# In the attention's steps, the products for the next row maxima follow the scores directly, and the values follow both

## The chip, the cores and the metric

The kernel runs on one core of one Trainium2 chip. The time is device microseconds of that core. A core has five engines that work side by side and each take their own instructions in order: TensorE (PE, matrix products, into PSUM), VectorE (DVE), the scalar engine (ACT), GpSimd (POOL) and the queue that starts copies (SP). [...]

## The reference

Two layers of a metaformer run over x of shape 2 x 256 x 64 x 64: attention by areas, a recurrence over 4096 tokens, a mixer, and eight experts. The change lies in the first of these parts. With the normalisations of the batch left out, it computes

```python
# x: (2, 256, 64, 64), normalised over channels; 4 areas of 1024 positions per image,
# 8 heads of 32 channels each
attn = jnp.einsum('bhdn,bhdm->bhnm', q, k) * hd ** (-0.5)
attn = jax.nn.softmax(attn, axis=-1)
o = jnp.einsum('bhdm,bhnm->bhdn', v, attn)
...
return _conv1x1_bn(o + pp, w_proj, pr_g, pr_b, pr_m, pr_v)   # pp: a 5 x 5 convolution of v, by channel
```

and adds the result to x. The softmax takes the maximum of each row off before the exponential.

## The kernel before

`area_attention` treats 8 areas (2 images x 4) of 1024 positions, each in two groups of four heads: 16 groups, `GROUPS`. A group has 16 steps (`t`), two halves `n` of 512 queries times 8 blocks `m` of 128 keys; the loop at L542 runs over all 256. The order of the instructions on each engine is written out by hand (`manual_schedule`): what the loop emits first runs first.

A step of the loop emits, in this order:

- `scores` (L347): for four heads side by side on TensorE, each on 32 of its 128 rows, a product that puts minus the row maximum in (L352) and the scores on top of it (L357). They land in two wide tiles, s0 for heads 0 and 1, s1 for heads 2 and 3. ACT then takes the exponential of each (L364), into SBUF.
- `values` (L374) of the step before (`pending`): its exponentials times v, by four heads side by side on TensorE's columns (L370), summed over 8 steps in the tile `av_o`. After the eighth, ACT copies the sum (L383).
- small works from the table `SMALL`: `place` (L290) at steps 1 and 9 (other steps in the first group) turns the maxima found, split into three bf16 parts by `join`, into rows with a product (L294), an ACT copy (L298) and four copies on the SP queue (L301).
- `maxima` (L265), ahead of time for the next group (for the one after it in the last two steps): four products of the same shape as the scores but with queries on the output's partitions (L270), in two wide tiles m0 and m1. VectorE reduces each to row maxima (L275). The table `AHEAD` has one such set a step, `AHEAD_FIRST` two in the first ten steps of group 0.
- a sum of two exponential tiles on POOL (L564), by which the softmax's sums need fewer products. It carries two dependencies by hand: on the last product of the `maxima` and on the VectorE operation that was marked last before them.
- taps of the 5 x 5 convolution on VectorE (L324), as many as `TAPS` says for the step.
- from the tables `MINE` and `AROUND` projections for the next groups, averages, transposes and the output (L166, L178, L239), which use a PSUM tile `po` with one buffer; `sums` (L385) in every fourth step; and from `LATE` and `LATE_AROUND` the vector work of the normalisation and of `join`. The normalisation's root takes a power on POOL (L203) in step 6 of an area's first group.

The wide tiles are two PSUM banks each and come from one pool with three buffers, which `scores` and `maxima` take in turn:

```python
ps1 = ctx.enter_context(tc.tile_pool(name="a_psum_1", bufs=3, space=PSUM))
...
def wide():
    return ps1.tile([P, 2, 512], F32, name="ps", tag="ps")
```

The exponentials' tiles have three buffers in even steps and one in odd steps (L363).

Of the kernel before, what the change touches and what calls it, by code (L numbers as in the profile page):

```python
# [93 lines left out]
def area_attention(tc, sh, ap):  # L94
# [13 lines left out]
    with ExitStack() as ctx:  # L108
# [39 lines left out]
        def wide():  # L148
            return ps1.tile([P, 2, 512], F32, name="ps", tag="ps")
# [108 lines left out]
        def head(h):  # L258
            return slice(HD * h, HD * h + HD)
# [5 lines left out]
        def maxima(G, at):  # L265

            i, n = CHUNKS[at]
            tiles = [wide(), wide()]
            for h in range(GH):
                mm = nc.tensor.matmul(  # L270
                    tiles[h // 2][:, h % 2], qs[G, i // HM][head(h), i % HM * P : (i % HM + 1) * P],
                    ks[G, n][head(h)], start=True, stop=True, tile_position=(HD * h, 0),
                )
            for j in range(2):
                nc.vector.tensor_reduce(  # L275
                    nms[G][:, n, 2 * j : 2 * j + 2, i], tiles[j], AX.X, ALU.max, negate=True
                )
            return mm.ins
# [27 lines left out]
        def taps(A):  # L306

            vh, a = vhs[A], AREAS[A][1]
            for lower in range(2):
                for c in range(2):  # L310
                    if not lower:
                        acc = accs[A, c] = p1.tile([P, AROWS, WW], F32, name=f"acc{c}")
                        nc.vector.tensor_scalar(
                            acc, vh[:, c, 2 : 2 + AROWS], w_pe[:, c, 12:13], t_pe[:, c : c + 1], ALU.mult, ALU.add
                        )
                        yield
                    for k in range(25):
                        dy, dx = k // 5 - 2, k % 5 - 2
                        if dy == 0 and dx == 0 or (dy > 0) != lower:
                            continue  # L320
                        r0, r1 = window(dy, AROWS, AROWS * a, HH)
                        w0, w1 = window(dx, WW)
                        part = accs[A, c][:, r0:r1, w0:w1]
                        mark(nc.vector.scalar_tensor_tensor(  # L324
                            part, vh[:, c, 2 + r0 + dy : 2 + r1 + dy, w0 + dx : w1 + dx],
                            w_pe[:, c, k : k + 1], part, ALU.mult, ALU.add,
                        ))
                        yield
# [18 lines left out]
        def scores(G, n, m):  # L347

            tiles, k = [wide(), wide()], ks[G, m // HM]
            for h in range(GH):  # L350
                at = slice(HD * h, HD * h + 3)
                nc.tensor.matmul(  # L352
                    tiles[h // 2][:, h % 2], ones_b[at], mxs[G, n][at],
                    start=True, stop=False, tile_position=(HD * h, 0),
                )
            for h in range(GH):
                nc.tensor.matmul(  # L357
                    tiles[h // 2][:, h % 2], k[head(h), m % HM * P : (m % HM + 1) * P], qs[G, n][head(h)],
                    start=False, stop=True, tile_position=(HD * h, 0),
                )  # L360
            exs = []
            for i in range(2):
                exs.append(pe.tile([P, 2, 512], F32, name=f"ex{i}{m % 2}", bufs=1 if m % 2 else 3))  # L363
                nc.scalar.activation(exs[i], tiles[i], AF.Exp, scale=HD**-0.5)  # L364
            return exs
# [3 lines left out]
        def on_columns(to, h, lhs, exs, first, last):  # L369
            nc.tensor.matmul(  # L370
                to[head(h)], lhs, exs[h // 2][:, h % 2], start=first, stop=last, tile_position=(0, HD * h)
            )

        def values(G, n, m, exs):  # L374
            A, c = GROUPS[G]
            if m == 0:
                values_of[0] = ps2.tile([P, 512], F32, name="av_o")
            for h in range(GH):
                on_columns(values_of[0], h, vts[A, c][:, m, head(h)], exs, m == 0, m == NM - 1)
            if m == NM - 1:  # L380
                if n == 0:
                    ys[A, c] = p3.tile([P, NA], F32, name="y")
                nc.scalar.copy(ys[A, c][:, HALVES[n]], values_of[0])  # L383

        def sums(G, n, half, pairs):  # L385

            ps = bank()
            for i, exs in enumerate(pairs):
                for h in range(GH):
                    on_columns(ps, h, ones, exs, i == 0, i == len(pairs) - 1)  # L390
            if half == 0:
                held["sum"] = p1.tile([P, 512], F32, name="sum")
                nc.scalar.copy(held["sum"], ps)
                return

            y, total = ys[GROUPS[G]][:, HALVES[n]], held.pop("sum")
            nc.vector.tensor_tensor(total, total, ps, ALU.add)
            turned = p1.tile([P, 512], F32, name="turned")
            nc.vector.transpose(turned, total)
            small = p1.tile([P, 512 // 32], F32, name="small")  # L400
            nc.vector.reciprocal(small, turned.rearrange("p (k i) -> p k i", i=32)[:, :, 0])
            nc.vector.transpose(
                total.rearrange("p (k i) -> p k i", i=32), small.unsqueeze(2).to_broadcast([P, 512 // 32, 32])
            )
            mark(nc.vector.tensor_tensor(y, y, total, ALU.mult))
# [123 lines left out]
        def works(G, t, *tables):  # L529

            A, c = GROUPS[G]
            mine, around = tables
            plan = [(f, G + k, a, len(GROUPS)) for k, f, *a in mine.get(t, ())]
            plan += [(f, A + k, a, len(AREAS)) for k, f, *a in around.get(t, ())]
            for f, at, a, end in plan:
                if 0 <= at < end:
                    f(at, *a)

        pending, due, pairs, odd = None, {}, [], None
        at_end = mybir.DependencyInfo(mybir.DependencyClass.Sync, mybir.DependencyReason.DATA)  # L540
        conv = iter(())
        for g in range(16 * len(GROUPS)):  # L542
            G, t = divmod(g, 16)
            A, c = GROUPS[G]
            n, m = divmod(t, NM)
            new = G == 0
            if t == 0 and c == 0:
                conv = taps(A)
            exs = scores(G, n, m)
            if pending is not None:  # L550
                values(*pending)
            works(G, t, SMALL_FIRST if new else SMALL, {})

            mm, before = None, latest[0]
            for k, at in (AHEAD_FIRST if new else AHEAD).get(t, ()):
                if G + k < len(GROUPS):
                    mm = maxima(G + k, at)
            pair = None
            if m % 2:
                pair = (pairs[-1][0], exs[0])  # L560
            elif odd is not None:
                pair = (pairs[-1][1], odd)
            if pair is not None:
                add = nc.gpsimd.tensor_tensor(pair[0], *pair, ALU.add)  # L564
                if mm is not None:
                    tc.add_manual_dep(add.ins, mm.name, at_end, reason="beside the reductions")
                    tc.add_manual_dep(add.ins, before.name, at_end, reason="beside the reductions")
            for _ in range((TAPS_FIRST if A == 0 else TAPS)[c][t]):
                next(conv, None)
            works(G, t, FIRST if new else MINE, AROUND[c])  # L570
            if g in due:
                sums(*due.pop(g))
            works(G, t, LATE_FIRST if new else LATE, LATE_AROUND_FIRST if new else LATE_AROUND[c])
            pending = G, n, m, exs
            if m % 2:
                odd = exs[1]
                if m % 4 == 3:
                    due[g + 2] = G, n, m // 4, pairs
                    pairs = pairs[-1:]
            else:  # L580
                pairs = (pairs if m % 4 else []) + [exs]
# [1677 lines left out]
```

## Time and profile before

| what | us |
|---|---|
| median of 2 runs (3005.82 and 3010.76) | 3008.29 |
| the profiled execution, its own time | 3003.18 |
| span of its instructions | 3001.4 |
| steps of the attention, from the first L352 to the end of the last step | about 63 to 1465 |
| recurrence, mixer and experts | from about 1498 on |

The profile gives for each engine a record of every instruction. A group of equal instructions is named by its line, its engine and its tiles, "written<-read"; PEld is the weight load that goes ahead of a product. An fp32 product stands there as two records, two passes. The view of waits names who waited for whom; idle time of an engine costs something only where the end depends on it. TensorE's ends are modelled, so the distance from one start to the next is safer to read than a length.

### The profile page before, as it was taken

What the parts mean: (1) busy time and instruction counts of PE and PEld (TensorE: products, weight loads), DVE (VectorE), ACT (ScalarE), POOL (GpSimd) and SP (SyncE); (2) the same over time, 40 slices, a digit from 0 to 9 for tenths busy, and PEclk for the clock granted to TensorE, in tenths of its full rate; (3) what the DMA queues carried; (4) which work ended last, traced back from release to release, by engine and by line L of the source; (5) the groups of instructions that cost most, each with busy time, mean ns of one, the idle gap of its engine ahead of it and who ended that gap; (6) DMA issues with size and microseconds to landing.
All of it is one profiled execution on the core that took longest, in us unless ns stands there. A gap on an engine that the chain in (4) does not pass through costs nothing. (4 is left out here: it accounts for less than half of the span.)

```text
span 3001.4 us, 45442 instructions
## 1 busy us (share of the span) xinstructions
PE 2724.7 (91%) x17798; PEld 1512.9 (50%) x17798; DVE 2173.2 (72%) x3227; ACT 1348.5 (45%) x2417; POOL 1358.1 (45%) x1037
## 2 busy tenths in 40 slices
PE   7999999999999999998689999968887499999994
PEld 2222232333323333322189999953444378888872
DVE  4799898999989999998766667779987812222116
ACT  3344444454544445444344455556753822222223
POOL 1444545554454555546523000038773256666651
PEclk9999999999999999999899999989999799999995
DMA  3000000000000000000023000005552456666658
GB/s 127 1 1 1 1 1 1 1 1 1 1 1 1 1 1 1 2 1 1 2 104 148 1 2 1 1 24 152 149 141 57 166 184 230 228 224 228 225 178 339
DMA packets 58659, 220.34 MB, mean 73 GB/s; under 512 B 14440, under 2 KB 15344, under 8 KB 48704
## 3 DMA queue, kind: packets, MB, share of 16 engines
q0 software_dynamic: 25440, 125.24, 11.7%
q1 hardware_dynamic: 31760, 87.82, 8.9%
q10 hardware_dynamic: 1232, 4.25, 0.4%
q8 instruction: 142, 2.33, 0.3%
q14 instruction: 85, 0.70, 0.1%
HBM read 173.30 MB, written 43.58 MB: 72 GB/s over the span
## 5 line engine op out<-in xcount | busy, mean ns | idle before, releaser
L564 POOL TENSOR_TENSOR ex<-ex,ex 128x1024 f32<-128x1024 f32 x255 | 617.3, 2425 | 615.1 <-PE ps L270 248.9
L275 DVE TENSOR_REDUCE nm<-ps 128x2 f32<-128x1024 f32 x512 | 601.3, 1219 | 91.2 <-PE ps L270 90.5
L364 ACT ACTIVATE ex<-ps 128x1024 f32<-128x1024 f32 x512 | 498.0, 1022 | 318.2 <-PE ps L357 285.5
L324 DVE SCALAR_TENSOR_TENSOR acc<-vh,w_pe,acc 128x1008 f32<-128x1008 f32 (+7 forms) x384 | 548.9, 1431 | 7.1
L270 PE MATMUL ps<-k,q 32*128 32x512 f32 x2048 | 348.0, 647 | 4.9 <-DVE nm L275 3.6
L2003 DVE COPY xt<-px 128x512 f32<-128x512 f32 x68 | 47.0, 692 | 398.0 <-PE px L2001 398.0
L2015 ACT ACTIVATE act<-ph,wt 128x256 f32<-128x256 f32 x272 | 128.8, 474 | 395.8 <-PE ph L2013 373.0
L2013 PE MATMUL ph<-xt,wt 128*128 128x256 f32 x1088 | 291.8, 391 | 5.2 <-ACT act L2015 2.5
L357 PE MATMUL ps<-q,k 32*128 32x512 f32 x2048 | 286.8, 606 | 0.0
L370 PE MATMUL av_o<-ex,vt 128*32 128x512 f32 x2048 | 280.8, 615 | 4.8 <-ACT ex L364 4.6
L2023 PE MATMUL py<-wt,act 128*128 128x256 f32 x1088 | 278.7, 379 | 0.0
L270 PEld LDWEIGHTS ps<-k,q 32*128 32x128 f32 x2048 | 122.8, 185 | 209.7 <-issue 85.5
L2013 PEld LDWEIGHTS ph<-xt,wt 128*128 128x128 f32 x1088 | 190.5, 191 | 68.5 <-DVE xt L2003 23.9
L771 PE MATMUL z<-xs,u 128*128 128x128 f32 x1872 | 222.2, 275 | 0.8 <-ACT xs L751 0.8
L771 PEld LDWEIGHTS z<-xs,u 128*128 128x128 f32 x1872 | 215.7, 192 | 1.0 <-ACT xs L751 1.0
L2023 PEld LDWEIGHTS py<-wt,act 128*128 128x128 f32 x1088 | 201.6, 190 | 24.7
L795 ACT ACTIVATE t<-z,bias 128x128 f32<-128x128 f32 x468 | 136.3, 361 | 145.3 <-PE z L783 145.2
L2038 POOL DMA_INDIRECT results<-y,ri x136 | 138.0, 1015 | 139.5 <-DVE y L2031 100.7
L783 PE MATMUL z<-xs,v 128*128 128x128 f32 x1512 | 180.0, 275 | 0.1
L783 PEld LDWEIGHTS z<-xs,v 128*128 128x128 f32 x1512 | 174.2, 192 | 0.7 <-DVE xs L802 0.7
L1505 POOL TENSOR_TENSOR cs<-hs,cs 128x1024 f32<-128x1024 f32 x63 | 148.8, 2364 | 53.5 <-DVE hs L1498 33.3
L352 PE MATMUL ps<-mx,ones_b 3*128 3x512 bf16 x1024 | 132.4, 386 | 37.2 <-DVE nm L275 35.0
(419 smaller groups left out, 3791.0 us busy)
## 6 DMA issues: line engine op xcount, KB each, us to landing
cs<-c_rows SPq DMA_DIRECT2D x128, 256.0 KB
y<-results SPq DMA_DIRECT2D x32, 512.0 KB
x<-xrows SPq DMA_DIRECT2D x8, 1024.0 KB
rows<-xt SPq DMA_DIRECT2D x16, 512.0 KB
out_x<-res POOLq DMA_DIRECT2D x15, 512.0 KB
xrows<-xn SPq DMA_DIRECT2D x24, 256.0 KB
x<-in_x SPq DMA_DIRECT2D x4, 1024.0 KB
x<-in_x ACTq DMA_DIRECT2D x4, 1024.0 KB
```

What stands on the lines that cost most here:

```text
L270: mm = nc.tensor.matmul(tiles[h // 2][:, h % 2], qs[G, i // HM][head(h), i % HM * P : (i % HM + 1) * P], ks[G, n][head(h)], start=True, st ...
L275: nc.vector.tensor_reduce(nms[G][:, n, 2 * j : 2 * j + 2, i], tiles[j], AX.X, ALU.max, negate=True)
L324: mark(nc.vector.scalar_tensor_tensor(part, vh[:, c, 2 + r0 + dy : 2 + r1 + dy, w0 + dx : w1 + dx], w_pe[:, c, k : k + 1], part, ALU.mult, ...
L357: nc.tensor.matmul(tiles[h // 2][:, h % 2], k[head(h), m % HM * P : (m % HM + 1) * P], qs[G, n][head(h)], start=False, stop=True, tile_pos ...
L364: nc.scalar.activation(exs[i], tiles[i], AF.Exp, scale=HD**-0.5)
L370: nc.tensor.matmul(to[head(h)], lhs, exs[h // 2][:, h % 2], start=first, stop=last, tile_position=(0, HD * h))
L564: add = nc.gpsimd.tensor_tensor(pair[0], *pair, ALU.add)
L771: nc.tensor.matmul(z[c][:, g, :m], u[:, k, c, g], xt[:, k], start=g == GATES[0] and k == 0, stop=False, skip_group_check=True,)
L783: nc.tensor.matmul(z[c][:, g, :m], v[:, k, c, g], h[:, k], start=False, stop=k == 1, skip_group_check=True,)
L1505: nc.gpsimd.tensor_tensor(now["c", n], hs, now["c", n], ALU.mult)
L2013: nc.tensor.matmul(ph[:, hc], wt[:, at : at + P], xt[:, c], start=c == 0, stop=c == 1)
L2023: nc.tensor.matmul(py[:, j], act[:, hc, j * P : j * P + P], wt[:, at : at + C], start=hc == 0, stop=hc == NH - 1,)
```

## The change

Two lines of the loop move: `values` of the step before is emitted behind `maxima` instead of behind `scores`. `SMALL` works keep their place ahead of `maxima`, so that `place`, where there is one, now comes between the scores and the maxima without the values. The sum on POOL is still emitted after both. No instruction is added, dropped or resized, and no pool changes.

```diff
             exs = scores(G, n, m)
-            if pending is not None:
-                values(*pending)
             works(G, t, SMALL_FIRST if new else SMALL, {})
 
             mm, before = None, latest[0]
             for k, at in (AHEAD_FIRST if new else AHEAD).get(t, ()):
                 if G + k < len(GROUPS):
                     mm = maxima(G + k, at)
+            if pending is not None:
+                values(*pending)
             pair = None
```

## The prediction

> **What bounds the kernel now.** I read the busy times by slice first, then the stretch of the attention alone, then one step of it as a timeline, then the waits.
>
> In the slices of the page the attention is slices 1 to 20; the profiled span is 3001.4 us. TensorE (PE) and VectorE (DVE) both stand at 8 or 9 tenths there, DMA at nothing:
>
> ```profile
> span 3001.4 us, 45442 instructions
> ...
> PE   7999999999999999998689999968887499999994
> DVE  4799898999989999998766667779987812222116
> ...
> PEclk9999999999999999999899999989999799999995
> ```
>
> The stretches view for the steps that matter, 175 to 1392 us (columns: stretch, length, then PE, PEld, DVE, ACT, POOL busy, clock, DMA): PE is busy 1171 of 1217 us, DVE 1134, at a granted clock of 0.99. Two engines are near their end, so the order of one step must tell which waits for which.
>
> ```profile
> 175.00:1392.00 1217.00, 1170.90 (x7777) 367.18 (x7776) 1134.41 (x1030) 590.56 (x699) 610.73 (x365) 0.99 0.01 1
> ```
>
> One ordinary step in the timeline of PE (start, length, line):
>
> ```profile
> 706.77 0.40 PE L352 MATMUL ps<-mx,ones_b 3*128 3x512 bf16 x4
> 707.00 1.03 PE L357 MATMUL ps<-q,k 32*128 32x512 f32 x8
> 707.95 1.06 PE L370 MATMUL av_o<-ex,vt 128*32 128x512 f32 x8
> 708.95 1.38 PE L270 MATMUL ps<-k,q 32*128 32x512 f32 x8
> 710.26 1.98 PE L166 MATMUL po<-xn,wk 128*128 128x512 f32 x4
> ```
>
> The starts give the prices: row maxima into the scores (L352) 0.23 us, scores (L357) 0.95, values (L370) 1.00, products for the maxima (L270) 1.31, four projections (L166) 1.92. The next step starts at 712.18, so 5.41 us without a gap. Scalar engine (ACT) and VectorE in the same step:
>
> ```profile
> 708.13 1.94 ACT L364 ACTIVATE ex<-ps 128x1024 f32<-128x1024 f32 x2 [0.47 <-PE ps L357]
> ```
> ```profile
> 707.05 4.14 DVE L324 SCALAR_TENSOR_TENSOR acc<-vh,w_pe,acc 128x1008 f32<-128x1008 f32 x3
> 711.11 1.22 DVE L275 TENSOR_REDUCE nm<-ps 128x2 f32<-128x1024 f32 x1
> ```
>
> The point is in L270. The wide PSUM tiles rotate through three buffers and a step takes four: scores s0, s1, then m0, m1 for the maxima. Hence m1 lies in the buffer of s0 and must wait until the first exponential of the **same** step has read it; m0 lies in the buffer of the previous m1, and the next s1 in that of m0 (both wait for a reduction, L275). Single records of the trace: m0 starts at 708.95, the first exponential runs 708.13 to 709.15, m1 starts at 709.20, 1.08 us after that exponential began. Counted from the start of L357, the exponential begins at 1.07 to 1.13 in undisturbed steps and m1 at 2.15 to 2.21. Today L370 fills this time: m0 starts at 1.95, so m1 is late by 0.2 to 0.3 us only.
>
> The waits between 100 and 1500 us show what else stops a step (waiter, released by: sum, times, longest):
>
> ```profile
> PE ps L352 <- DVE nm L275: 34.6, 46, 2.2
> ...
> ACT ex L364 <- POOL ex L564: 32.6, 18, 5.8
> ```
>
> **The Trainium skill.** "TensorE: Matmul & The Clock Gate", section "Part 2: What happens when you issue a matmul", says that matmuls stay in program order and only weight loads are pulled ahead. The trace agrees: nothing of L166 starts before the last m1 product. So whatever stands behind m1 waits with it. "Perfetto Trace Analysis", section "Optimizing Tensor Performance", asks for independent groups to rotate through PSUM banks so that the emptying of one lies beside the next group's products; with three buffers for four tiles that works here because L370, which writes another tile, lies between. "TensorEngine Tiling (Array Packing)", section "Key Properties", says that a change of tiling mode drains TensorE. The trace shows 0.52 to 0.54 us from the last pass of one kind to the next kind, against 0.43 to 0.45 between the passes of one kind: some 0.1 us a change. "SBUF — State Buffer", section "Who interferes with whom", says that a VectorE instruction with two SBUF inputs contends with GpSimd's reads and a reduction never does. The trace agrees: L275 takes 1.22 us beside a GpSimd sum (POOL) or not; taps (L324) average 1.24 us without overlap and 1.81 where they lie mostly beside one.
>
> **The change, part by part.** The listing of instructions shows the same rows on DVE, ACT and POOL, and on PE only the move of L370 behind L270; on SP only a tile's number changes, its copies keep their order. Nothing is added or removed. The loop has 238 steps with maxima: 16 in group 0 (ten with two sets), 222 later. The last 18 have none and stay as they are.
>
> *The wait that is uncovered.* New order from the start of L357: m0 can start at 0.96; m1 still at about 2.18 (scores end and the exponential takes what it takes); its second pass 0.43 later; values 0.52 after that, at 3.13; they take 0.99, so the next kind starts at 4.12. Today an undisturbed step gets there at 3.20 (its 5.35 less 0.23 for L352 and 1.92 for the projections). **Cost 0.92 us a step.** m0 runs inside the wait on half of the array's rows, so it pays for nothing. Queued behind m1 on PE are the values, the projections and the next scores; all shift, and ACT and DVE with them. 222 x 0.92 = **+204 us**. Could the values' removal from this place spare a mode change? Once a step at most, 0.1 us, x222 = 22: this is in the range, not the sum, since m1 is late by its exponential whatever the mode.
>
> *The waits that go.* An undisturbed step takes 5.35 us where projections, averages or sums follow (187 of the 222), 4.02 where four transposes follow (28), 3.29 where nothing does (7): together 1136 us. The 222 steps really take 1217 (175.2 to 1392.2), so **81 us** are disturbance. Of it 42 us is s1 held back by the reduction of m0 (the sum of what L352 to L357 takes beyond 0.23), about 24 us lie in step 9 of six groups (8.3 to 9.9 us instead of 5.35) and the step after one of them, where ACT waits for POOL to free an exponential's buffer behind a power (L203) of 5.46 us; the other 15 are steps whose products for the maxima or whose exponential came late. With values between m1 and the next s1, a reduction has 1 us more; with 0.9 us more in each step DVE (84 to 87 us per 16 steps) and POOL fall behind a PE that now needs 14 x 6.27 + 2 x 4.94 = 97.7. In step 9 the power starts in step 6, so three steps give 2.7 us for a stall of 2.9 to 4.5. I take 71 of the 81 as gone and leave 10.
>
> *Who is late next.* The POOL sum (L564) is released by the last L270 product. In odd steps it also overwrites a tile which the moved values still read, so it starts about 1 us later in the step, at 4.4 us from its start, when the reductions (2.3 to 4.7) are nearly over: it moves beside the taps. Overlapped taps advance at 1.24/1.81 = 0.69 of their pace, so 2.6 us of overlap cost 0.8 us of DVE; today's overlap is 0.6 us a sum. At 8 odd steps a group that is 6 us, even ones half of it: DVE goes from 87 to at most 96 per 16 steps, still under 97.7. I cost it at nothing, with PE as cover; if the cover is gone, +30 us. The copy of the finished values (L383) sits on ACT behind both exponentials and waits 2 us longer in every eighth step; the next ACT work there, a projection's copy, is only ready at the step's end, so nothing. `place` (L294) now follows the scores by itself at 1.19 us; its bank is freed by an ACT copy which ends about 0.9 after the step's start: nothing, 0.25 us of margin.
>
> *Group 0.* Its ten double steps run m0, m1, m0', m1'; m1' waits for the first reduction. New: m0's reduction ends at 3.3, m1' starts at 3.35, values end at 5.35, against 5.47 today: -1 us in ten. The six single steps cost 6 x 0.92, less 2.4 us of a wait that goes: +3. Together **+2 us**.
>
> *Tail.* From 1392 us DVE finishes the taps of the last area and nothing of that order changes: it ends as much later as the last reductions. The recurrence and the experts, half of the span, are untouched.
>
> Sum: 204 - 71 + 2 = **+135 us** on the profiled execution's own 3003.18 us: 3138. The two runs shown have 3005.8 and 3010.8 (median 3008.3), 5 us above the profiled one; I take **3140 us**, +4.4%.
>
> **Rivals.**
> 1. *Slower, and DVE with it* (chance 0.08): the sums beside the taps cost 2 us per odd step, DVE needs 87 + 16 = 103 per group and binds: 5.3 x 14 = 74 more, 3214. For it: DVE is at 93% today. Against: a late DVE puts its reductions back beside the sums, which undoes the overlap.
> 2. *No difference* (0.05): m1 costs only what it exceeds the end of m0 by, 2.18 - 1.92 = 0.26, with values sliding into m0's half-empty time: 222 x 0.26 - 71 = -13, about 2993. Against: products stay in order, and values stand behind m1.
> 3. *Faster* (0.03): earlier reductions free DVE and the tiles, and the wait for the exponential is not paid at all, because TensorE already has another product in flight. Then the 71 to 81 us of disturbance is the whole effect: about 2930. It decides where the cost per step is under 81/222 = 0.36 us; a gain of 2% needs under 0.1. For it: PE waits for L275 in 46 places now. Against: m1 is seen to wait for its exponential even with values before it.
> That the change doesn't do what it says is excluded by the listing.
>
> **Numbers.** The forecast has 0.84. Its own ends: 0.70 us a step (mode change spared, m1's passes overlapping m0's) gives 3090; the POOL stalls kept (24) and the cover gone (+30) give about 3190. That range holds it 8 in 10 and needs no rival. Within 2% is 60 us, about what a measurement can tell here. Faster 0.03, within 2% 0.05, slower 0.92.
>
> **What would show it.** Right: L270 begins 0.96 us after L357 and spans about 2.1 us, with PE waiting for ACT ex L364 before its second half in over 200 steps; ordinary steps of 6.25 us instead of 5.35; the waits of L352 for L275 gone; step 9 without its stall; attention ending about 135 us later, the rest alike. Wrong: ordinary steps under 5.7 us (rival 2 or 3), or L352 still waiting for L275 with longer taps (rival 1).

## The result and the profile after

The changed kernel takes 3157.85 us (median of 2 runs, 3155.01 to 3160.68) against 3008.29 us before: ratio 1.0505, 95% interval 1.0469 to 1.0541, so 150 us slower. Its profiled execution has a span of 3153.2 us, 151.8 us more than before.

From the page of the changed kernel, the span and the slices (tenths busy):

```profile
span 3153.2 us, 45443 instructions
...
PE   8999999999999999999859999996888589999994
DVE  5899999999999999999876666678987832222115
PEclk9999999999999999999979999998999789999995
```

Read alone, these lines tempt to a wrong conclusion: both engines are busier, and VectorE's busy total on the page went from 2173.2 to 2325.3 us, by 152.1, the very amount by which the kernel became slower. Which engine sets the step is not in a busy share. The stretches view of the changed kernel for the same steps as before (the 222 that carry one set of maxima, from the second group on; columns as in the prediction) has 1365 us where the kernel before had 1217:

```profile
171.00:1536.00 1365.00, 1302.83 (x7776) 406.73 (x7774) 1279.80 (x1029) 591.19 (x699) 602.90 (x364) 1.00 0.00 1
```

One ordinary step of the changed kernel, from TensorE's timeline:

```profile
767.46 0.39 PE L352 MATMUL ps<-mx,ones_b 3*128 3x512 bf16 x4
767.68 1.03 PE L357 MATMUL ps<-q,k 32*128 32x512 f32 x8
768.55 1.02 PE L270 MATMUL ps<-k,q 32*128 32x512 f32 x4
769.84 1.13 PE L270 MATMUL ps<-k,q 32*128 32x512 f32 x4 [0.27 <-ACT ex L364]
770.89 1.06 PE L370 MATMUL av_o<-ex,vt 128*32 128x512 f32 x8
771.89 1.55 PE L166 MATMUL po<-xn,wq 128*128 128x512 f32 x3
```

and ACT's exponentials in it:

```profile
768.76 1.94 ACT L364 ACTIVATE ex<-ps 128x1024 f32<-128x1024 f32 x2 [0.42 <-PE ps L357]
```

L270 is now split in two. m0 starts at 768.55, 0.87 us after L357; m1 starts at 769.84, 1.08 us after the first exponential, as before, and PE names ACT as the one that held it. Before, the eight products started over 0.8 us and the next kind came 1.31 us after the first; here it comes 2.34 us after it. The whole step takes 6.34 us in place of 5.35 in an undisturbed step before.

The waits of the changed kernel between 100 and 1650 us (waiter, released by: sum, times, longest):

```profile
PEld ps L270 <- ACT ex L364: 252.3, 237, 1.4
...
PE ps L270 <- ACT ex L364: 58.6, 193, 0.6
...
ACT ex L364 <- POOL ex L564: 12.6, 5, 5.7
...
PE ps L352 <- DVE nm L275: 6.0, 6, 1.7
```

The first line is new: 237 times the weight load of m1 waits for the exponential, where the kernel before had 11 such waits and 4.4 us. Counted over the whole trace, every one of the 238 steps with maxima has it (the ten steps with two sets twice; a few of them lie before 100 us). PE's own idle time, 58.6 us, is only a part of the loss, since m0 still runs during the wait, on half of the array's rows. The last two lines were, before, 32.6 us in 18 places and 34.6 us in 46: the waits that the prediction let go have nearly gone, and they are worth far less than the new one. The page's lines of the two VectorE groups show what moved there: a tap's mean is 1754 ns instead of 1431, a reduction's 1218 instead of 1219.

```profile
L324 DVE SCALAR_TENSOR_TENSOR acc<-vh,w_pe,acc 128x1008 f32<-128x1008 f32 (+7 forms) x384 | 672.7, 1754 | 7.1
L275 DVE TENSOR_REDUCE nm<-ps 128x2 f32<-128x1024 f32 x512 | 604.0, 1218 | 62.4 <-PE ps L270 60.0
```

Where the 151.8 us of the span lie, from the starts of the steps in both traces:

| stretch | before | after | difference |
|---|---|---|---|
| up to the first step | 62.7 | 62.0 | -0.7 |
| group 0 (two sets of maxima in ten steps) | 112.5 | 107.7 | -4.8 |
| 222 steps with one set | 1217.0 | 1365.9 | +148.9 |
| steps without maxima, end of the attention | 105.9 | 108.1 | +2.2 |
| recurrence, mixer, experts | 1503.3 | 1509.5 | +6.2 |

The last row is not a part of the change: in the nine other kernels below it lies between 1501 and 1510 us.

### The profile page after: what moved, and what is told of

Same layout as the page of the kernel before. It is cut to its first block, busy times and chain, and to the rows that moved or that the text cites. A ratio compares the mean times of both kernels' runs of the same rounds, so it can differ in the third digit from the quotient of the medians.

```text
span 3153.2 us, 45443 instructions
## 1 busy us (share of the span) xinstructions
PE 2863.1 (91%) x17798; PEld 1559.3 (49%) x17798; DVE 2325.3 (74%) x3227; ACT 1349.3 (43%) x2417; POOL 1352.4 (43%) x1037
## 5 line engine op out<-in xcount | busy, mean ns | idle before, releaser
L324 DVE SCALAR_TENSOR_TENSOR acc<-vh,w_pe,acc 128x1008 f32<-128x1008 f32 (+7 forms) x384 | 672.7, 1754 | 7.1
L275 DVE TENSOR_REDUCE nm<-ps 128x2 f32<-128x1024 f32 x512 | 604.0, 1218 | 62.4 <-PE ps L270 60.0
L270 PE MATMUL ps<-k,q 32*128 32x512 f32 x2048 | 539.1, 623 | 63.2 <-ACT ex L364 60.4
L270 PEld LDWEIGHTS ps<-k,q 32*128 32x128 f32 x2048 | 165.4, 184 | 378.4 <-ACT ex L364 262.1
L357 PE MATMUL ps<-q,k 32*128 32x512 f32 x2048 | 269.7, 592 | 0.0
L1857 POOL DMA_INDIRECT xg<-rows,xi x136 | 130.2, 957 | 76.9 <-issue 76.6
```

The lines of the kernel that those rows point to most:

```text
L270: mm = nc.tensor.matmul(tiles[h // 2][:, h % 2], qs[G, i // HM][head(h), i % HM * P : (i % HM + 1) * P], ks[G, n][head(h)], start=True, st ...
L275: nc.vector.tensor_reduce(nms[G][:, n, 2 * j : 2 * j + 2, i], tiles[j], AX.X, ALU.max, negate=True)
L324: mark(nc.vector.scalar_tensor_tensor(part, vh[:, c, 2 + r0 + dy : 2 + r1 + dy, w0 + dx : w1 + dx], w_pe[:, c, k : k + 1], part, ALU.mult, ...
L357: nc.tensor.matmul(tiles[h // 2][:, h % 2], k[head(h), m % HM * P : (m % HM + 1) * P], qs[G, n][head(h)], start=False, stop=True, tile_pos ...
```

## The experiments

Two theories. **W**: m1 waits for the exponential that empties its PSUM buffer, with nothing left to fill the time. **P**: the sums on POOL now lie beside the taps, and VectorE's growth is the cause. Each experiment starts from the changed kernel ("after") or from the one before, and its ratio is to runs of the kernel before on the same chip (medians 2996 to 3010 us there). A line "..." in an edit stands for parts left out. "222 steps" is the time from the first exponential of step 16 to that of step 238 (1216.4 us before, 1365.9 after).

### The second exponential first (after)

```diff
-            exs = []
-            for i in range(2):
-                exs.append(pe.tile(...))
+            exs = [pe.tile(...)
+                   for i in range(2)]
+            for i in (1, 0):
                 nc.scalar.activation(exs[i], tiles[i], AF.Exp, scale=HD**-0.5)
```

> Theory W (the second half of the maxima's products, m1, waits for the exponential that empties its PSUM buffer): the exponential of s0 now comes second, ends 0.92 us later, and m1 with it. Ordinary steps 6.34 -> 7.26 us, 222 of them: +204 us against the changed kernel, about 3360 us. Theory P (the sums on POOL now lie beside the taps, and VectorE, whose busy time rose by 152 us, is what grew): nothing in that changes, 3150 to 3160 us.

Measured: 3169.65 us, ratio 1.0533 (1.0492 to 1.0574); 222 steps 1378.6 us. The expectation of W failed, but by a mistake in the experiment. In the trace m1 still starts 1.08 us after the first exponential of the step, which is now that of s1. The trace names no buffers; it fits a pool that hands m1 the buffer which comes free first. So the run does not delay m1 as it was meant to, and says nothing for either theory but that m1 follows whichever exponential comes first: that one begins 1.19 us after L357 instead of 1.13 (medians), and the 222 steps take 13 us more.

### The first exponential twice (after)

To delay it in fact, the first exponential is computed twice into the same tile:

```diff
-            for i in range(2):
-                exs.append(pe.tile(...))
+            for i in (0, 0, 1):
+                if i == len(exs): exs.append(pe.tile(...))
                 nc.scalar.activation(exs[i], tiles[i], AF.Exp, scale=HD**-0.5)
```

> The changed kernel with the first exponential of each step computed twice into the same tile, so that s0 is given free 0.92 us later. Theory W: m1 moves by that much; ordinary steps 6.34 -> 7.26 us, 222 of them, +204 us: about 3360 us. Theory P: ACT has time for it (43% busy), under 3175 us.

Measured: 3525.87 us, ratio 1.1758 (1.1720 to 1.1796). P is out by 350 us, W by 166. TensorE's timeline of this kernel:

```profile
863.69 1.03 PE L357 MATMUL ps<-q,k 32*128 32x512 f32 x8
864.55 1.02 PE L270 MATMUL ps<-k,q 32*128 32x512 f32 x4
866.95 1.13 PE L270 MATMUL ps<-k,q 32*128 32x512 f32 x4 [1.38 <-ACT ex L364]
868.01 1.49 PE L370 MATMUL av_o<-ex,vt 128*32 128x512 f32 x8
869.43 3.21 PE L166 MATMUL po<-y,wpr 128*128 128x512 f32 x4
```

m1 starts 3.26 us after L357 instead of 2.21 (the median over the 222 steps 3.26 against 2.21), and an undisturbed step with projections takes 7.40 us instead of 6.34: all of the delay arrives in the step. That is 222 x 1.06 = 235 us. The 222 steps took 354 us more (1720.3 us), so some 119 us are not this wait. The last two lines show where some of them are: the values take 1.42 us from start to start instead of 1.00 and four projections 3.14 instead of 1.92. The stretches view shows the clock there:

```profile
860.00:868.00 8.00, 6.62 (x36) 1.92 (x32) 7.41 (x6) 3.90 (x5) 3.75 (x5) 1.00 0.00 0
868.00:873.00 5.00, 5.00 (x22) 1.75 (x24) 2.40 (x2) 0.32 (x1) 5.00 (x2) 0.66 0.00 0
```

The granted clock falls to 0.66 in these five us; over the stretch from 171 to 1914 us it is 0.91 to 0.93, where it was 0.99 and 1.00 in the kernels before and after. In the 222 steps its mean is 0.92, which is worth at most 0.08 x 1720 = 138 us (an estimate, as if TensorE had work all the time): it can be the whole of the 119.

### No sums on POOL, in both orders

The sum of two exponential tiles is left out, so that POOL has little left beside VectorE's taps, and the softmax's sums lack part of their terms.

```diff
-                add = nc.gpsimd.tensor_tensor(pair[0], *pair, ALU.add)
-                if mm is not None:
+                add = None
+                if add is not None:
...
-        nc.gpsimd.tensor_tensor(pairs[-1][1], pairs[-1][1], odd, ALU.add)
```

In the changed kernel:

> The changed kernel without the sums on POOL (the softmax's sums lack part of their terms). Theory W: steps keep 6.34 us, since m1's wait is unchanged; only a few disturbed steps in the first groups may shorten: 3140 to 3160 us, with VectorE's busy time back near 2150. Theory P: the time goes back with the contention, to 3010 us or below.

In the kernel before:

> The kernel before without the sums on POOL (the softmax's sums lack part of their terms), the base for the changed kernel without them (3113 us). Theory W: with the contention gone from both, the change still costs 222 steps of 0.9 to 1.0 us plus the stalls that it would otherwise spare (step 9 has none without sums): this base is at 2900 to 2940 us, the distance 170 to 210 us. Theory P: without the sums both orders cost the same, so this base is near 3110 us.

Measured: 3112.98 us (ratio 1.0344, 1.0302 to 1.0387) and 2936.43 us (ratio 0.9796, 0.9760 to 0.9832). Without any sums the change costs 176.5 us, more than with them; the two runs were on different chips, but by the traces' 222 steps it is 176.5 us too. A tap's mean is the same in the two, 1241 and 1240 ns:

```profile
L324 DVE SCALAR_TENSOR_TENSOR acc<-vh,w_pe,acc 128x1008 f32<-128x1008 f32 (+7 forms) x384 | 475.9, 1241 | 7.1
```
```profile
L324 DVE SCALAR_TENSOR_TENSOR acc<-vh,w_pe,acc 128x1008 f32<-128x1008 f32 (+7 forms) x384 | 475.3, 1240 | 7.1
```

(the changed kernel without sums first, then the one before without them). The 222 steps take 1355.4 and 1178.9 us. Against the changed kernel itself only 10.5 us went from its 222 steps, and an undisturbed step has 6.34 us with the sums or without; 34 of the 45 us that the first of these runs gained lie in the steps without maxima, where the order was not changed, and the kernel before without sums gained 30 us there too. So the changed kernel met neither expected time (W, with 3140 to 3160, had left out these last steps), while the kernel before and the distance came as W had them. P explains at most about 10 of the 149 us. Of the kernel before, the sums cost 37.5 us in the 222 steps.

### The sums behind the reductions (before)

The overlap alone, in the order of the kernel before:

```diff
...
-                nc.vector.tensor_reduce(
+                reduced[0] = nc.vector.tensor_reduce(
...
-                    tc.add_manual_dep(add.ins, before.name, at_end, reason="beside the reductions")
+                    tc.add_manual_dep(add.ins, reduced[0].name, at_end, reason="behind the reductions")
```

> The order of the kernel before, but each sum on POOL waits for the second reduction of its step, so that it lies beside the taps. It has the overlap of the changed kernel without m1's wait. Theory P: this alone brings most of the 150 us, 3120 to 3160. Theory W (the overlap is cost that TensorE's longer steps covered in the changed kernel): in this order nothing covers it, VectorE has 86 us of 86 to 90 per 16 steps and rises by about 8: some 3080 to 3130 us, with TensorE waiting for reductions (L352 for L275) and not for the exponential.

Measured: 3310.37 us, ratio 1.1039 (1.1004 to 1.1074); 222 steps 1508.1 us: 150 us above the higher of the two expectations. A tap's mean rises to 2066 ns. In the waits between 100 and 1600 us L352 waits for L275 133 times, ACT for POOL 108 times:

```profile
POOL ex L564 <- DVE nm L275: 701.5, 211, 6.7
...
ACT ex L364 <- POOL ex L564: 202.4, 108, 2.3
...
PE ps L352 <- DVE nm L275: 155.4, 133, 4.4
```

The full overlap is thus dear in the old order: VectorE is busy 1429 of the 1503 us from 187 to 1690 us, and I had priced only the longer taps, not the exponentials that wait for a late sum. A part of the time is not the overlap itself: the granted clock is 0.94 in that stretch, worth at most 0.06 x 1503 = 90 us (an estimate) of the 292 by which the 222 steps grew. The run does not contradict the runs without sums: in the changed kernel 0.97 us of tap time lies beside a sum on average, here 2.08, and its longer steps leave VectorE the time. That last clause is an argument; the run itself shows only what the full overlap costs in the old order.

### Values between the halves of the maxima (after)

```diff
             for h in range(GH):
+                if h == 2 and between is not None: values(*between)
                 mm = nc.tensor.matmul(
...
-                    mm = maxima(G + k, at)
+                    mm, pending = maxima(G + k, at, pending), None
```

> Values between the two halves of the maxima: m0, values, m1. m1 no longer waits for its exponential. Theory W with the half-empty array (each half of the maxima uses 64 of 128 rows and no longer runs beside the other): m0 at 0.86 after the scores' start, values at 1.81, m1 at 2.81, next at 3.8 us, against 4.27 in the changed kernel and 3.20 before: ordinary steps 5.95 us, about 3065 us. If the wait alone cost the time: back to the kernel before, about 3010 us. Theory P: the sums start right after m1, later than in the kernel before by little; 3010 to 3050 us.

Measured: 3123.27 us, ratio 1.0379 (1.0338 to 1.0419); 222 steps 1328.6 us. None of the numbers was met. TensorE's timeline:

```profile
767.40 1.03 PE L357 MATMUL ps<-q,k 32*128 32x512 f32 x8
768.26 1.02 PE L270 MATMUL ps<-k,q 32*128 32x512 f32 x4
769.21 1.06 PE L370 MATMUL av_o<-ex,vt 128*32 128x512 f32 x8
770.21 1.13 PE L270 MATMUL ps<-k,q 32*128 32x512 f32 x4
771.27 1.13 PE L166 MATMUL po<-xn,wq 128*128 128x512 f32 x2
```

m1 does not wait for its exponential any more, TensorE has no gap, and still the step takes 6.01 us (expected: 5.95). Each half of the maxima takes about a microsecond by itself (0.95 and 1.06), the two together took 1.31 where they ran side by side. So the 1.0 us a step of the change are two losses: 0.3 us in which TensorE has nothing, which this order gives back, and some 0.7 us in which it works with half of its rows. Removing the idle time alone does not bring the old time. The 222 steps have 55 us more than their undisturbed lengths add up to; in three stretches of 7 to 20 us, 37 us together, the granted clock was 0.5, which is worth up to 19 of them (an estimate).

### Four orders: what covers the exponential, what covers the reduction

A step has two places where TensorE depends on a tile being emptied: m1 on the first exponential, which follows the scores, and the next s1 on the reduction of m0, which follows the maxima. And it has two independent pieces to put there: the values and the works (projections, averages, transposes). In the 12 of 16 steps that have works, two more orders were built, the first from the changed kernel, the second from the one before. Works between scores and maxima, values behind:

```diff
             exs = scores(G, n, m)
+            large = not new and (t in MINE or t in AROUND[c])
+            works(G, t, MINE if large else {}, AROUND[c] if large else {})
+            if pending is not None and not large: values(*pending)
...
-            if pending is not None:
+            if large:
                 values(*pending)
...
-            works(G, t, FIRST if new else MINE, AROUND[c])
+            works(G, t, FIRST if new else {} if large else MINE, {} if large else AROUND[c])
```

> In the 12 of 16 steps with projections, averages or transposes, these stand between the scores and the maxima, and the values stay behind the maxima; the other four steps have the old order. Theory W: the works cover the exponential as the values did, both halves of the maxima start together, TensorE needs about 5.05 us a step (some 81 us per 16), so VectorE binds with 85 to 88 us per 16 steps: 2980 to 3005 us, a little under the kernel before. Theory P: the sums still wait for the values in every odd step and lie beside the taps: VectorE rises as in the changed kernel, above 3080 us.

and works and values both ahead of the maxima, which have nothing behind them:

```diff
             exs = scores(G, n, m)
+            large = not new and (t in MINE or t in AROUND[c])
+            works(G, t, MINE if large else {}, AROUND[c] if large else {})
             if pending is not None:
                 values(*pending)
...
-            works(G, t, FIRST if new else MINE, AROUND[c])
+            works(G, t, FIRST if new else {} if large else MINE, {} if large else AROUND[c])
```

> The order scores, works, values, maxima in the 12 of 16 steps with works, the old one in the rest: m1 is covered twice, and the sums start behind the last product of the maxima as in the kernel before. Theory W: TensorE packs both halves of the maxima side by side (0.25 us a step less), VectorE binds with 85 to 89 us per 16 steps, and the next s1 has to wait for m0's reduction: 2985 to 3015 us. Theory P: no overlap is added, so no change, 3000 to 3015 us; the two differ little here, the trace of the steps decides.

| order | covers the exponential | covers the reduction | us | 222 steps |
|---|---|---|---|---|
| before | values | works | 3008 | 1216.4 |
| works between | works | values | 3044.95 | 1250.2 |
| works first | works and values | nothing | 3149.69 | 1356.4 |
| the change | nothing | values and works | 3157.85 | 1365.9 |

The ratios are 1.0123 (1.0090 to 1.0155) for works between and 1.0507 (1.0479 to 1.0534) for works first. Both expectations failed. Works first was expected at 2985 to 3015: its order saves 0.35 us at the maxima and loses four times as much, because s1 now stands right behind m1. TensorE's timeline of works first:

```profile
760.50 0.38 PE L352 MATMUL ps<-mx,ones_b 3*128 3x512 bf16 x2
761.99 0.39 PE L352 MATMUL ps<-mx,ones_b 3*128 3x512 bf16 x2 [1.11 <-DVE nm L275]
762.00 1.25 PE L357 MATMUL ps<-q,k 32*128 32x512 f32 x8
763.17 1.98 PE L166 MATMUL po<-xn,wk 128*128 128x512 f32 x4
765.09 1.06 PE L370 MATMUL av_o<-ex,vt 128*32 128x512 f32 x8
766.08 1.14 PE L270 MATMUL ps<-k,q 32*128 32x512 f32 x8
767.04 0.38 PE L352 MATMUL ps<-mx,ones_b 3*128 3x512 bf16 x2
```

L270 is packed (0.96 us to the next start), and 1.11 us of idle time stand before the second half of L352, with the reduction as its releaser; the scores, from the first L352 to the next kind, take 2.67 us instead of 1.18. Works between was expected at 2980 to 3005 (W) or above 3080 (P). It gives back 116 of the 149 us of the 222 steps, though its sums also wait for the values: 50 of POOL's waits, 195.3 us, end on them, and a tap's mean is 1472 ns, near the 1431 of before. It stays 34 us behind the kernel before in these steps. Its reduction is covered by the values' 1.00 us only. TensorE idles for it hardly longer than before (38.0 us in 78 places, against 34.6 in 46), but the products of s1 now start behind those of s0, as m1's did behind m0's:

```profile
700.05 0.78 PE L352 MATMUL ps<-mx,ones_b 3*128 3x512 bf16 x4
700.44 1.25 PE L357 MATMUL ps<-q,k 32*128 32x512 f32 x8
701.62 1.98 PE L166 MATMUL po<-xn,wk 128*128 128x512 f32 x4
```

The scores take 1.57 us here instead of 1.18. Over the 222 steps they take 47 us more than in the kernel before, of which the shorter maxima give back 17: nearly all of the 34.

### The power in two halves (before)

A side question, whether the stalls in step 9 were the power on POOL:

```diff
-                3: [(1, square, 1)], 6: [(1, root, 0)],
-                8: [(1, root, 1), (1, scale, 0)], ...
+                3: [(1, square, 1)], 5: [(1, root, 0, HALVES[0])], 7: [(1, root, 0, HALVES[1])],
+                8: [(1, root, 1, at) for at in HALVES] + [(1, scale, 0)], ...
...
```

> The kernel before with the root of the normalisation in two halves, at steps 5 and 7 instead of whole at step 6: two powers of about 2.8 us on POOL instead of one of 5.46. If the stalls of step 9 (about 24 us in six groups) come from sums that queue behind the power, they go: about 2985 us. If a late sum is held by something else, no change: 3005 us.

Measured: 3001.12 us, ratio 0.9996 (0.9978 to 1.0015): no difference. The stall is smaller in step 9 and comes back ahead of it: in group 6, for one, step 9 is 3.30 us shorter, steps 7 and 8 are 1.42 and 0.63 longer. Over the six groups about 2 us are left. The power does hold the sums up, as the moved stall shows; its halves, 2.93 us each instead of 5.46, held up others. No order tried here beats the kernel before.

## Why the prediction was right

The forecast was +135 us on the profiled execution; it was +151.8 on the span. Of the 17 us between them, the second step below has 10, the third 6, group 0 -7; the rest lies outside the steps with maxima, most of it in the recurrence and the experts, where the kernels differ by up to 9 us among themselves. By its steps:

1. *m1 stays at its exponential.* Right: m1 starts 1.08 us after the exponential begins, as before. Where the exponential is computed twice, it starts 1.08 us after the second copy begins.
2. *0.92 us a step, 204 us.* The mechanism was right, the term a little too small. The undisturbed steps of the changed kernel are 6.34 us with projections or averages (131 steps), 6.21 with sums (56), 5.02 with transposes (28), 4.43 with nothing (7): together 1350 us against 1136 before, **+214 us**, 0.96 a step. From m1 to the values it takes 1.06 us, where the prediction had 0.43 + 0.52 = 0.95, since it put m1's second pass 0.43 us behind its first. It comes 0.53 behind (769.84 and 770.37). The change did not bring this: in the kernel before m1's passes start at 709.20 and 709.74, and the projections follow 1.06 us after m1 there too. The prediction had misread that trace, where it put 0.43 to 0.45 us between all passes of one kind. In both traces the distance is 0.53 where the first pass starts together with its weight load of 0.18 us: m1 behind its wait, but also the projections and, before, m0 behind the values, which waited for nothing. It is 0.43 where the load ran ahead (m0 in the changed kernel: load at 768.12, product at 768.55). Two other small terms went the way the prediction named as possible: m0 starts at 0.87 instead of 0.96 behind scores of the same tiling, which the wait hides, and steps in which sums follow the values, which share a tiling too, are 0.13 us shorter.
3. *71 of the 81 us of disturbance go.* 65 went: 16 us are left above the undisturbed steps. L352's waits are down to 6.0 us and the stall of step 9 is gone as said.
4. *The sums beside the taps at nothing.* Right for the 222 steps within about 10 us (with the sums against without: 10.5). How much the taps grow came out nearly right too, but by luck. They took 124 us more in all, 0.49 us a sum; the prediction had 0.8 in odd steps and half of it in even ones. Its two factors were both off. It took the taps' pace beside a sum as 0.69, from a mean of 1.81 us, but in the kernel before the 33 taps that lie by more than half beside a sum take 2.65 us. And the overlap grew from 0.48 to 0.97 us a sum, not to 2.6. The Trainium skill's page "SBUF — State Buffer" (section "Who interferes with whom") states that a VectorE instruction with two SBUF inputs contends with GpSimd's reads; the taps agree, with a mean of 1241 ns without sums and 1754 with them. That TensorE covers the longer taps was the right part of the argument. Where it does not, with all sums beside the taps in the old order, the run took 300 us more, its lower clock included; the prediction allowed +30 for that.
5. *Group 0, +2 us.* It was -4.8: the ten steps with two sets went from 79.8 to 70.4 us, where the prediction had only 1 us, since it had counted the undisturbed steps (7.6 to 7.4) and not the three that were stalled before (steps 4, 8 and 9, 30.1 to 22.4 us). The six others cost 4.6.
6. *The rivals.* None took place. The second (m1 costs only what it exceeds m0 by) had 0.26 us a step, and TensorE's idle time is just that, 0.27; it fell because m0 and m1, apart, take about a microsecond each, and the values stand behind both. The run with values between the halves shows both parts.

## What to carry to other kernels

An instruction that fills time on an in-order engine is worth what it covers. Before moving it, list for each tile the last reader that must let go of it, and see what stands between; and look for products that run side by side and come apart when one of them has to wait, for that cost more here (0.7 us) than the idle time (0.3 us). With three buffers for four tiles this step has two such places, and the independent pieces have to be shared out between them: all on one side lost 140 or 149 us at the other, as the four orders show. Busy time that grows by exactly the time lost need not be the cause: take the suspected work out of both versions and look at the difference again.

## What the runs showed of the hardware that was not expected

Two products on 64 of the 128 rows take about as long as four on all of them (0.95 us for one half of the maxima alone, 0.96 for both side by side). A first pass of the maxima or the projections that starts together with its weight load, behind a wait or behind a product of another kind, has its second pass 0.53 us behind it; m0 in the changed kernel, whose load ran ahead, has 0.43. A VectorE tap that lies by more than half beside a POOL sum takes 2.65 us in the kernel before instead of 1.24, while a reduction stays at 1.22. And TensorE's granted clock fell in two kernels, to 0.92 where the exponential was doubled and 0.94 where the sums lay behind the reductions: the trace has it at 0.5 for 3.4 or 6.8 us at a time, the first of the two for 276 us of its 222 steps. TensorE idled for 289 and 235 us of these steps, never for more than 1.6 us in one piece in the first; the kernel with works first idled for 199 us and stayed at 1.00, and the one with values between the halves, which idled for 12, had 37 us at 0.5. What sets it wasn't tried.
